# Merged SP transfers and a written SP order in an adaLN block with delta-rule attention and a mixture of experts

## The chip, the cores and the metric

The kernel runs on one core of a Trainium2 chip. The metric is the device time of one execution in microseconds. Lower is better.

The core has five engines that run at the same time, each with its own list of instructions, taken strictly in order: PE (matrix products; its weight loads are listed apart as PEld), DVE (vector work), ACT (activations), POOL (general elementwise work and indirect transfers) and SP, which here does nothing but begin transfers. A transfer is begun by an instruction on an engine's list, is carried out by 16 DMA engines that the whole core shares, and tells by a semaphore that it has landed. An instruction that waits for a semaphore holds up all that stands behind it on its engine.

## The reference

For x of 4 sequences of 1024 tokens with 256 features (all float32):

```python
mod = (_silu(L0_c) @ L0_wmod).reshape(B, 6, 1, -1)         # shifts, scales, gates sa ca ga sb cb gb
h = _layernorm(x) * (1 + ca) + sa
x = x + ga * attention(h)
h = _layernorm(x) * (1 + cb) + sb
x = x + gb * moe(h)

# attention: 16 heads of 64; q, k, v are projected, run through a causal convolution of 4 taps and silu
k = k / max(norm(k), 1e-12);  alpha = sigmoid(h Wa + ba);  beta = sigmoid(h Wb + bb)
def step(S, xs):                                           # a scan over the 1024 tokens
    v_old = S @ kt
    upd = vt - at * v_old
    S = clip(at * S + bt * outer(upd, kt), -5.0, 5.0)
    return S, S @ qt
y = y * silu(h Wg + bg);  out = y Wo

# moe: 8 experts of width 512, the two best of each token, softmax over the two, gelu
```

## The kernel before, in words

The scan is worked in chunks of 32 tokens of all four sequences (128 rows, `nch` = 32 chunks). Two chunks make a pair, and there are 16 pairs (`npair`). The function `chunks` runs over the pairs: while the two chunks of one pair pass through the recurrent state `S` (class `Chunk`), the next pair is prepared (class `Pair`). After the last pair, `blocks` runs the experts. Further functions (`rest`, `steps`, `experts`) stand behind conditions that are not met with these inputs.

The parts of a pair's work are Python generators, each with a letter: `k` keys and queries, `v` values and gates, `t` the triangular system, `s` the scaling of keys and queries (`scaled`), `c` the passes of the chunks with `outputs` and `finish`, `b` the bounds, `x` the loads of later rows of x, `z` the clearing of rows for the experts, and so on. The string `PLAN` gives the order in which they are advanced by one `yield` each, once a pair. That order is the written order. Line 379 sets `manual_schedule` for PE, DVE, ACT and POOL: their instructions stand in the program as written. SP is not in that set: there, a scheduler places the transfers by its own estimate of when each can begin.

All of the following transfers are begun on SP in the part that `chunks` builds, and their names are those in the profile:

- `w_kq`, `w_v`, `w_gt` (L428, L433, L436): the projections' weights, loaded anew in every pair from `in_w_qkv` and `in_w_g`, two head pairs ahead of their use. Each buffer is one of three (`w_kq`, `w_v`) or four (`w_gt`), so a load waits for the last product with the weights that lay there. `load_kq` makes two transfers, one for keys and one for queries, and `load_v` one for `w_v` and two for `w_gt`. `project` (L610) takes the weights, an activation (L619) begins the convolution, and three operations of DVE for each (L628) end it.
- `x` (L423): a chunk's rows of x. They are wanted in the order (sequence, half, token) and lie in HBM as (half, sequence, token), so `fill_x` makes eight transfers of 16 rows. Chunks 0 to 5 are loaded at the start, the others in `loads`, four chunks ahead of their pair's pass.
- `spread` to `g_scratch` (L900): the growth factors of a pair, which DVE makes in `triangle` (L894, L895), are written to HBM in four transfers, one for each sequence.
- `sc` from `g_scratch` (L994): in `scaled` they are read back, each row sent to 64 partitions. This happens four times a pair (queries and keys, even and odd chunk), with two transfers of 64 partitions each. POOL then multiplies (L1001), in two operations of 512 columns each, and copies `last` (L1004). `at_heads` gives the place in HBM.
- `x_scratch`, `out` (L1280, L1283): in `finish` a chunk's x after attention, which POOL has added (L1278), is stored, and then copied to `out` from HBM to HBM, its rows put in the other order.
- `u_scratch` (L1297) and `growth_scratch` (L735, L837): stores for the bounds.
- `rows_scratch` from `zero_row` (L1338): `clear` fills the experts' lists with blank rows, in 128-row parts, 18 parts a pair.

In the passes, POOL's `decayed` (L1231) makes `aS`, DVE adds the new part to it and gets `S` (L1196), and DVE's `yT` (L1252) takes the outputs out of PSUM.

The three buffers for PSUM results of most matmuls (`bank`) are taken in turn, so a product also waits until the one three before it has been read.

Of the kernel before, what the change touches and what calls it, by code (L numbers as in the profile page):

```python
# [32 lines left out]
F32 = mybir.dt.float32  # L33
# [3 lines left out]
ALU = mybir.AluOpType  # L37
# [3 lines left out]
B, D, C, NH, DH, KC = 4, 256, 1024, 16, 64, 4  # L41
HP = NH // 2
TC, TH, TE = 32, 16, 8
# [3 lines left out]
P = 128  # L47
RW = D + 8
# [313 lines left out]
def chunks(ctx, tc, a, nch, con, ones, modt, modc, x1_dram, rt, out):  # L362

    nc = tc.nc
    GA, SB, CB, GB = range(4)
    ident, iota8 = con["ident"], con["iota8"]
    npair = nch // 2
    wp = ctx.enter_context(tc.tile_pool(name="c_w", bufs=1))
    bp = ctx.enter_context(tc.tile_pool(name="c_buf", bufs=1))
    s1 = ctx.enter_context(tc.tile_pool(name="c_one", bufs=1))  # L370
    s2 = ctx.enter_context(tc.tile_pool(name="c_two", bufs=2))
    s3 = ctx.enter_context(tc.tile_pool(name="c_thr", bufs=3))
# [3 lines left out]


    E = mybir.EngineType
    ctx.enter_context(tc.manual_schedule(engines={E.PE, E.DVE, E.Activation, E.Pool}))

    is_open, done = {}, set()

    def take(pool, shape, name, tag=None, bufs=1, **more):
        tag = tag or name
        assert is_open.get(tag, 0) < bufs, tag
        is_open[tag] = is_open.get(tag, 0) + 1
        if bufs > 1:
            more["bufs"] = bufs
        return pool.tile(shape, F32, name=name, tag=tag, **more)

    def close(*tags):
        for tag in tags:
            is_open[tag] -= 1
            assert is_open[tag] >= 0, tag

    def need(*what):
        assert done.issuperset(what), what
# [3 lines left out]
    def bank(shape, name):  # L401
        banks[0] += 1
        return ps_g.tile(shape, F32, name=name, tag=f"g{banks[0] % 3}")

    half_p = lambda p: slice(p * 64, p * 64 + 64)
    quads = [slice(b * 32, b * 32 + 32) for b in range(B)]
# [6 lines left out]
    QC, KK, VC = 0, 1, 2  # L413

    x_of = {}

    def load_x(c, eng=nc.sync):
        x_of[c] = take(s3, [P, D], "x", bufs=9)
        fill_x(c, x_of[c], eng)

    def fill_x(c, x, eng):
        for there, here in by_batch(a["x"][c], x):
            eng.dma_start(here, there)  # L423

    def load_kq(hp):
        w = s3.tile([P, 2, 2, P], F32, name="w_kq")
        for x, i in ((KK, 0), (QC, 1)):
            nc.sync.dma_start(w[:, :, i], a["w_qkv"][:, :, x, hp])  # L428
        return w

    def load_v(hp):
        w = s3.tile([P, 2, P], F32, name="w_v", bufs=3)
        nc.sync.dma_start(w, a["w_qkv"][:, :, VC, hp])  # L433
        wg = s3.tile([P, 2, P], F32, name="w_gt", bufs=4)
        for p in range(2):
            nc.sync.dma_start(wg[:, :, half_p(p)], a["w_g"][:, :, p, hp * DH : (hp + 1) * DH])  # L436
        return w, wg

    w_next, v_next = [], []
# [166 lines left out]
    def project(w, h_t, x, hp, o):  # L606

        ps = bank([P, 2 * B, KC - 1 + TC], "ps_q")
        for dc in range(2):
            nc.tensor.matmul(  # L610
                ps.rearrange("p y t -> p (y t)"),
                lhsT=w[:, dc],
                rhs=h_t[:, dc].rearrange("p x b t -> p (x b t)"),
                start=(dc == 0),
                stop=(dc == 1),
            )
        taps = conv[:, x, hp]
        o = o.rearrange("p x b t -> p (x b) t")
        nc.scalar.activation(  # L619
            o, ps[:, :, 0:TC], AF.Identity, scale=taps[:, 0:1], bias=taps[:, KC : KC + 1]  # L620
        )
        return ps, taps, o

    def convolve(*projected):

        for j in range(1, KC):
            for ps, taps, o in projected:
                nc.vector.scalar_tensor_tensor(  # L628
                    o, ps[:, :, j : j + TC], taps[:, j : j + 1], o, op0=ALU.mult, op1=ALU.add
                )  # L630

    def silu(f):
        f = f.rearrange("p h x b t -> p (h x b t)")
        nc.scalar.activation(f, f, AF.Silu)

    def idle(n):
        for _ in range(n):
            yield

    class Pair:  # L640
# [100 lines left out]
        def keys_and_queries(self):  # L741
            need(("h", self.g), ("halo", self.g))
            kq = self.kq = take(s2, [P, 2, HP, 2, B, TC], "kq", bufs=2)
            for hp in range(HP):
                w = w_next.pop(0)
                w_next.append(load_kq((hp + 2) % HP))
                two = []
                for x, i in ((KK, 0), (QC, 1)):
                    two.append(project(w[:, :, i], self.h_t, x, hp, kq[:, i, hp]))
                    yield  # L750
                convolve(*two)
                yield
                if hp % 2:
                    for i in range(2):
                        silu(kq[:, i, hp - 1 : hp + 1])
                        if i and hp == HP - 1:
                            done.add(("kq", self.g))
                        yield
# [81 lines left out]
        def triangle(self):  # L840

            g, kq, dec, gam = self.g, self.kq, self.dec, self.gam
            need(("kq", g), ("dec", g))

            kk_r = self.kk_r = take(s1, [P, 32, TC], "kk_r")
            dq = self.dq = take(s2, [P, 32, TC], "dq", bufs=2)
            for par in range(2):
                two = [bank([P, HP, 2, TC], "ps_kk") for _ in range(2)]
                at = banks[0]
# [20 lines left out]
            kk = take(s1, [P, TC, TC], "kk")  # L870
# [22 lines left out]
            spread = s2.tile([P, 2, TC], F32, name="spread")  # L893
# [2 lines left out]
                spread[:, 0], spread[:, 1], -1.0, rk, op0=ALU.mult, op1=ALU.mult  # L896
            )

            for b, q in enumerate(quads):
                nc.sync.dma_start(g_dram[g][:, :, b].rearrange("w n t -> n w t"), spread[q])  # L900
            done.add(("spread", g))
            w_t = s1.tile([P, TC], F32, name="w_t")
            nc.vector.tensor_tensor(w_t, be, rk, ALU.mult)
# [27 lines left out]
            for x in range(2):  # L931
                at = [slice(x * TH + y * TE, x * TH + (y + 1) * TE) for y in range(2)]
# [45 lines left out]
        def scaled(self):  # L978


            g, kq = self.g, self.kq
            need(("M", g))
            kd = self.kd = take(s1, [P, 32, TC], "kd", tag="gam")
            nc.gpsimd.tensor_tensor(kd, self.dec, self.kk_r, ALU.mult)
            close("kk_r")
            yield
            need(("kt", g), ("spread", g))
            close("arep")
            self.last = []
            for w in (1, 0):  # L990
                for par in range(2):
                    sc = take(s1, [P, HP, B, TC], "sc", tag=("kk", "kk_r")[par])
                    for p in range(2):
                        nc.sync.dma_start(  # L994
                            sc[half_p(p)].rearrange("q h b t -> q (h b t)"),
                            at_heads(g, w, p, par).partition_broadcast(DH),
                        )
                    yield
                    for h4 in range(0, HP, 4):
                        o = kq[:, w, h4 : h4 + 4, par]  # L1000
                        nc.gpsimd.tensor_tensor(o, o, sc[:, h4 : h4 + 4], ALU.mult)  # L1001
                    if w == 1:
                        last = take(s3, [P, B, HP], "last", bufs=3)
                        nc.gpsimd.tensor_copy(last.rearrange("q b h -> q h b"), sc[:, :, :, TC - 1])  # L1004
                        self.last.append(last)
                    close(("kk", "kk_r")[par])
                    if (w, par) == (0, 1):
                        done.add(("scaled", g))
                    yield
# [38 lines left out]
    def at_heads(g, w, p, par):  # L1048

        n = p * 16 + par * 8  # L1050
        return g_dram[g][w, n : n + 8].rearrange("n b t -> (n b t)")

    def of_pair(w, g):

# [271 lines left out]
            yield  # L1326


    g_dram = nc.dram_tensor("g_scratch", [npair, 2, 32, B, TC], F32, kind="Internal").ap()

    rows = rt.rows[: NE * rt.room].rearrange("(e n p) d -> n p e d", e=NE, p=P)
    blank = iter([(n, e) for n in range(nch + BL // P) for e in range(NE)])
    blanks = []

    def clear(count):

        for _, (n, e) in zip(range(count), blank):
            one = nc.sync.dma_start(rows[n][:, e], rt.zero)  # L1338
            for other in rt.sent:
                apart(tc, one, other)  # L1340
            blanks.append((n, one))

    def clears():
        for _ in range(6):
# [45 lines left out]

    def loads(first):
        for c in range(first, min(first + 2, nch)):
            load_x(c)
            yield

    def both_of(pair, prev):
# [75 lines left out]
    def later_loads():  # L1472

        yield from idle(1)
        for c, x in unread:
            fill_x(c, x, nc.sync)
            yield
            if c > 2:
                yield
        nc.sync.dma_start(rw, a["router"])  # L1480
        for p in range(2):
            for x in range(2):
                nc.sync.dma_start(
                    w_o[half_p(p)].rearrange("q (h x) d -> q x h d", x=2)[:, x],
                    a["w_o"][half_p(x), :, p],
                )
        yield
# [17 lines left out]
    for g in range(npair):  # L1505
# [4 lines left out]
        if g + 1 < npair:  # L1510
            x = newer
# [895 lines left out]
```

## Time and profile before

| | |
|---|---|
| time, median of 3 executions | 1919.11 us (1913.41 to 1926.53) |
| the profiled execution: time, span | 1922.9 us, 1921.1 us |
| mean granted clock of TensorE | 0.919 |
| busy: PE, PEld, DVE, ACT, POOL | 1632.0, 1297.1, 1482.3, 826.7, 716.4 us |
| transfers begun on SP, largest groups | rows_scratch 272, w_kq 260, w_gt 260, x 248, w_v 130, sc 128, u_scratch 128 |
| moved by the DMA engines | 249.52 MB, mean 130 GB/s |

The profile is of one execution. The span goes from the first instruction to the last, and the time of an execution is a little more. A line of the timeline or of a group names the source line, the engine, the operation and its tiles (out<-in); a line of SP (SPq) is an instruction that begins a transfer, and its length is the time it holds the queue, not the time until the data have landed. In brackets stands how long the engine was idle before and what, as far as the semaphores tell, ended that. A line of waits says who waited for whom: microseconds in total, how often, and the longest.

### The profile page before, as it was taken

To read this page: it belongs to the slowest core of one execution; us is meant where nothing else is said; L and a number is where in the kernel's file an instruction comes from. 1 tells how busy PE (TensorE), PEld (TensorE's weight loads), DVE (VectorE), ACT (ScalarE), POOL (GpSimd) and SP (SyncE) were. 2 spreads that over 40 slices of the span, in tenths; PEclk is the share of its full clock that TensorE was granted. 3 is DMA by queue.
4 is the path that set the end of the run, shared out by engine and by line. 5 is a ranking of instruction groups with operands and counts; after the bars stand their busy time and mean duration, and the time that the engine had idled before them with its cause. 6 is when DMAs were issued, how large, how long until landed. Compare 5 with 4: busy or idle time off the path is not lost.

```text
span 1921.1 us, 88201 instructions
## 1 busy us (share of the span) xinstructions
PE 1632.0 (85%) x38610; PEld 1297.1 (68%) x38610; DVE 1482.3 (77%) x3622; ACT 826.7 (43%) x1652; POOL 716.4 (37%) x913
## 2 busy tenths in 40 slices
PE   5578999889989898989898989898888675989994
PEld 3456676667676766767676767676667564878883
DVE  4678797968788888878787978797968335789973
ACT  3344545444545544545445444554443112334331
POOL 1032343424342525252534343433424432454343
PEclk9889998989999998989899989998989677999997
DMA  4455444443545445354535453636343216788882
GB/s 117 127 161 129 105 108 94 107 109 95 148 115 141 123 120 137 107 134 111 146 103 150 106 153 97 161 94 153 110 112 112 56 36 207 187 208 219 231 231 35
DMA packets 431490, 249.52 MB, mean 130 GB/s; under 512 B 242996, under 2 KB 410808, under 8 KB 430840
## 3 DMA queue, kind: packets, MB, share of 16 engines
q1 hardware_dynamic: 416488, 223.65, 43.6%
q0 software_dynamic: 13664, 18.38, 5.2%
q8 instruction: 306, 5.01, 1.1%
q10 hardware_dynamic: 944, 1.77, 0.3%
q14 instruction: 88, 0.72, 0.1%
HBM read 165.99 MB, written 81.87 MB: 129 GB/s over the span
## 4 chain that ended last, share of the span: by engine, by line
PE 66%; DVE 11%; issue 7%; POOL 5%; SPq 5%; DMA 4%; ACT 3%; POOLq 0%; DVEq 0%; ACTq 0%
PE ps_q L610 22%; PE ps_hm L2116 6%; PE ps_yb L2129 6%; PE ps_w L1265 5%; PE ps_gt L780 4%; PE ps_u L1149 3%; PE ps_kk L853 3%; PE ps_o L1208 2%; PE ps_z L1127 2%; SPq L423 2%; PE ps_t L1031 2%; PE ps_s L1187 2%; DMA sc<-g_scratch 2%; PE ps_t L1019 2%; DVE kq L628 2%
## 5 line engine op out<-in xcount | busy, mean ns | idle before, releaser
L628 DVE SCALAR_TENSOR_TENSOR kq<-ps_q,w_conv,kq 128x256 f32<-128x256 f32 x768 | 319.7, 476 | 150.2 <-ACT kq L619 149.6
L610 PE MATMUL ps_q<-hT,w_kq 128*128 128x280 f32 x1024 | 323.2, 460 | 58.9 <-issue 20.6
L610 PEld LDWEIGHTS ps_q<-hT,w_kq 128*128 128x128 f32 x1024 | 203.5, 213 | 125.9 <-issue 58.2
L619 ACT ACTIVATE kq<-ps_q,w_conv 128x256 f32<-128x256 f32 x256 | 142.4, 563 | 234.8 <-PE ps_q L610 233.1
L1001 POOL TENSOR_TENSOR kq<-kq,sc 128x512 f32<-128x512 f32 x128 | 163.5, 1299 | 143.6 <-DMA sc<-g_scratch 116.5
L2136 POOL DMA_INDIRECT out<-yb,at_b x72 | 120.4, 1672 | 190.2 <-DVE gate L2106 48.7
L628 DVE SCALAR_TENSOR_TENSOR v<-ps_q,w_conv,v 128x256 f32<-128x256 f32 x384 | 158.9, 476 | 41.9 <-ACT v L619 41.7
L1231 POOL TENSOR_TENSOR aS<-S,last 128x1024 f32<-128x1024 f32 x64 | 122.5, 1914 | 135.9 <-DVE S L1196 133.4
L780 PE MATMUL ps_gt<-hT,w_gt 128*128 128x256 f32 x512 | 144.3, 410 | 29.6 <-issue 20.5
L787 ACT ACTIVATE gate<-ps_gt,b_gt 128x256 f32<-128x256 f32 x128 | 60.5, 473 | 239.3 <-PE ps_gt L780 239.1
L610 PE MATMUL ps_q<-hT,w_v 128*128 128x280 f32 x512 | 153.5, 441 | 11.6 <-issue 4.7
L2116 PE MATMUL ps_hm<-hT,w 128*128 128x256 f32 x576 | 136.4, 392 | 7.6 <-issue 5.9
L2123 ACT ACTIVATE hm<-ps_hm,b 128x256 f32<-128x256 f32 x144 | 68.2, 474 | 167.5 <-issue 120.4
L2129 PE MATMUL ps_yb<-w,hm 128*128 128x256 f32 x576 | 130.3, 379 | 0.0
L2116 PEld LDWEIGHTS ps_hm<-hT,w 128*128 128x128 f32 x576 | 112.7, 197 | 25.9 <-issue 8.9
L610 PEld LDWEIGHTS ps_q<-hT,w_v 128*128 128x128 f32 x512 | 97.7, 204 | 47.3 <-issue 13.1
L780 PEld LDWEIGHTS ps_gt<-hT,w_gt 128*128 128x128 f32 x512 | 92.0, 194 | 53.1 <-issue 28.5
L1265 PE MATMUL ps_w<-w_o,yT 128*128 128x256 f32 x512 | 121.0, 391 | 4.3 <-DVE yT L1252 2.8
L1278 POOL TENSOR_TENSOR x<-x,add 128x256 f32<-128x256 f32 x32 | 29.0, 905 | 236.4 <-DVE add L1276 232.3
L2129 PEld LDWEIGHTS ps_yb<-w,hm 128*128 128x128 f32 x576 | 106.7, 190 | 13.4 <-DVE yb L2134 0.3
L1265 PEld LDWEIGHTS ps_w<-w_o,yT 128*128 128x128 f32 x512 | 98.2, 195 | 20.1 <-DVE yT L1252 3.0
L619 ACT ACTIVATE v<-ps_q,w_conv 128x256 f32<-128x256 f32 x128 | 71.3, 573 | 93.7 <-PE ps_q L610 93.7
(265 smaller groups left out, 3230.5 us busy)
## 6 DMA issues: line engine op xcount, KB each, us to landing
w<-in_w SPq DMA_DIRECT2D x72, 512.0 KB
rows_scratch<-zero_row SPq DMA_DIRECT2D x272, 132.0 KB
w_kq<-in_w_qkv SPq DMA_DIRECT2D x260, 128.0 KB
sc<-g_scratch SPq DMA_DIRECT2D x128, 256.0 KB
w_v<-in_w_qkv SPq DMA_DIRECT2D x130, 128.0 KB
w_gt<-in_w_g SPq DMA_DIRECT2D x260, 64.0 KB
u_scratch<-u SPq DMA_DIRECT2D x128, 128.0 KB
hb<-rows_scratch SPq DMA_DIRECT2D x36, 264.0 KB
```

Source lines behind the costliest of these rows:

```text
L610: nc.tensor.matmul(ps.rearrange("p y t -> p (y t)"), lhsT=w[:, dc], rhs=h_t[:, dc].rearrange("p x b t -> p (x b t)"), start=(dc == 0), sto ...
L619: nc.scalar.activation(o, ps[:, :, 0:TC], AF.Identity, scale=taps[:, 0:1], bias=taps[:, KC : KC + 1])
L628: nc.vector.scalar_tensor_tensor(o, ps[:, :, j : j + TC], taps[:, j : j + 1], o, op0=ALU.mult, op1=ALU.add)
L780: nc.tensor.matmul(ps, lhsT=wg[:, dc], rhs=self.h_t[:, dc, :, :, KC - 1 :].rearrange("p x b t -> p (x b) t"), start=(dc == 0), stop=(dc == 1),
L787: nc.scalar.activation(gate[:, hp].rearrange("p x b t -> p (x b t)"), ps.rearrange("p y t -> p (y t)"), AF.Silu, bias=b_gt[:, hp : hp + 1],)
L1001: nc.gpsimd.tensor_tensor(o, o, sc[:, h4 : h4 + 4], ALU.mult)
L1231: nc.gpsimd.tensor_tensor(aS.rearrange("q b h i -> q (b h) i"), S[:, bs].rearrange("q b h i -> q (b h) i"), self.pair.last[self.par][:, bs ...
L1265: nc.tensor.matmul(ps_w, lhsT=self.yT[:, hp].rearrange("q b t -> q (b t)"), rhs=w_o[:, hp], start=(hp == 0), stop=(hp == HP - 1),)
L2116: nc.tensor.matmul(ps, lhsT=self.w1[:, dc, fc * P : (fc + 1) * P], rhs=self.hT[:, dc], start=(dc == 0), stop=(dc == 1),)
L2123: nc.scalar.activation(self.hm[:, fc], ps, AF.Gelu, bias=self.b1[:, fc : fc + 1])
L2129: nc.tensor.matmul(ps, lhsT=self.hm[:, fc, s * P : (s + 1) * P], rhs=self.w2[:, fc], start=(fc == 0), stop=(fc == 3),)
L2136: return nc.gpsimd.indirect_dma_start(out=places, out_offset=bass.IndirectOffsetOnAxis(ap=self.at[:, s : s + 1], axis=0), in_=y, in_offset ...
```

## The change

SP joins the engines whose instructions stand in written order. Transfers are merged: one for `w_kq`, one for `w_gt`, one for `spread`, one for each run of blank rows that lie in the same 128-row part. From chunk 6 on, x is first copied from HBM to HBM in the wanted order (`reorder_x`, two chunks ahead of the load), and then loaded by one transfer. `g_scratch` now has the sequence ahead of the head, so that `spread` can go in one transfer; `sc` therefore lies as (sequence, head, token) in its 64 partitions and is filled in pieces of 1 KB, and POOL reads it with the two outer indices exchanged.

```diff
-    ctx.enter_context(tc.manual_schedule(engines={E.PE, E.DVE, E.Activation, E.Pool}))
+    ctx.enter_context(tc.manual_schedule(engines={E.PE, E.DVE, E.Activation, E.Pool, E.SP}))
...
+    x_rows = nc.dram_tensor("x_rows", [nch, P, D], F32, kind="Internal").ap()
+
+    def reorder_x(c):
+
+        if 6 <= c < nch:
+            nc.sync.dma_start(
+                x_rows[c].rearrange("(b h t) d -> b h (t d)", b=B, h=2),
+                a["x"][c].rearrange("(h b t) d -> b h (t d)", b=B, h=2),
+            )
+
     def load_kq(hp):
         w = s3.tile([P, 2, 2, P], F32, name="w_kq")
-        for x, i in ((KK, 0), (QC, 1)):
-            nc.sync.dma_start(w[:, :, i], a["w_qkv"][:, :, x, hp])
+        nc.sync.dma_start(w, a["w_qkv"][:, :, : KK + 1, hp])
         return w
...
-        for p in range(2):
-            nc.sync.dma_start(wg[:, :, half_p(p)], a["w_g"][:, :, p, hp * DH : (hp + 1) * DH])
+        nc.sync.dma_start(
+            wg.rearrange("x c (p i) -> x c p i", p=2), a["w_g"][:, :, :, hp * DH : (hp + 1) * DH]
+        )
...
-                    two.append(project(w[:, :, i], self.h_t, x, hp, kq[:, i, hp]))
+                    two.append(project(w[:, :, x], self.h_t, x, hp, kq[:, i, hp]))
...
-            for b, q in enumerate(quads):
-                nc.sync.dma_start(g_dram[g][:, :, b].rearrange("w n t -> n w t"), spread[q])
+            nc.sync.dma_start(g_dram[g].rearrange("w b n t -> (b n) w t"), spread)
...
-                    sc = take(s1, [P, HP, B, TC], "sc", tag=("kk", "kk_r")[par])
+                    sc = take(s1, [P, B, HP, TC], "sc", tag=("kk", "kk_r")[par])
                     for p in range(2):
                         nc.sync.dma_start(
-                            sc[half_p(p)].rearrange("q h b t -> q (h b t)"),
+                            sc[half_p(p)].rearrange("q b h t -> q b (h t)"),
                             at_heads(g, w, p, par).partition_broadcast(DH),
                         )
                     yield
                     for h4 in range(0, HP, 4):
                         o = kq[:, w, h4 : h4 + 4, par]
-                        nc.gpsimd.tensor_tensor(o, o, sc[:, h4 : h4 + 4], ALU.mult)
+                        nc.gpsimd.tensor_tensor(
+                            o, o, sc[:, :, h4 : h4 + 4].rearrange("q b h t -> q h b t"), ALU.mult
+                        )
...
-                        nc.gpsimd.tensor_copy(last.rearrange("q b h -> q h b"), sc[:, :, :, TC - 1])
+                        nc.gpsimd.tensor_copy(last, sc[:, :, :, TC - 1])
...
-        return g_dram[g][w, n : n + 8].rearrange("n b t -> (n b t)")
+        return g_dram[g][w, :, n : n + 8].rearrange("b n t -> b (n t)")
...
-    g_dram = nc.dram_tensor("g_scratch", [npair, 2, 32, B, TC], F32, kind="Internal").ap()
+    g_dram = nc.dram_tensor("g_scratch", [npair, 2, B, 32, TC], F32, kind="Internal").ap()
...
-        for _, (n, e) in zip(range(count), blank):
-            one = nc.sync.dma_start(rows[n][:, e], rt.zero)
+        some = [at for _, at in zip(range(count), blank)]
+        for n in sorted({n for n, _ in some}):
+            es = [e for m, e in some if m == n]
+            k = len(es)
+            one = nc.sync.dma_start(
+                rows[n][:, es[0] : es[0] + k], rt.zero.unsqueeze(1).to_broadcast([P, k, RW])
+            )
             for other in rt.sent:
                 apart(tc, one, other)
-            blanks.append((n, one))
+            blanks.extend([(n, one)] * k)
...
     def loads(first):
         for c in range(first, min(first + 2, nch)):
-            load_x(c)
+            reorder_x(c + 2)
+            x_of[c] = take(s3, [P, D], "x", bufs=9)
+            nc.sync.dma_start(x_of[c], x_rows[c])
             yield
...
         nc.sync.dma_start(rw, a["router"])
+        for c in (6, 7):
+            reorder_x(c)
         for p in range(2):
```

## The prediction

> **What bounds the kernel now.** I read the page first, for the engines' shares and the chain; then the waits, for who stops whom; then one pair of chunks instruction by instruction, on SP, POOL, DVE and PE; then the table by stage.
>
> ```profile
> span 1921.1 us, 88201 instructions
> ...
> PE 1632.0 (85%) x38610; PEld 1297.1 (68%) x38610; DVE 1482.3 (77%) x3622; ACT 826.7 (43%) x1652; POOL 716.4 (37%) x913
> ...
> PE 66%; DVE 11%; issue 7%; POOL 5%; SPq 5%; DMA 4%; ACT 3%; POOLq 0%; DVEq 0%; ACTq 0%
> ```
>
> PE carries two thirds of the chain, the SP queue and DMA 9% together (some 170 us). Chain shares are no savings: behind a removed link stands whatever was nearly as late. Hence the stage. Fifteen stretches of about 91 us (130 to 1495 us) each handle one pair; this is pair 7, for which the columns are the length and then the busy times of PE, PEld, DVE, ACT and POOL:
>
> ```profile
> 672.00:764.00 92.00, 83.30 (x2298) 64.62 (x2298) 74.92 (x182) 44.25 (x87) 36.27 (x50) 0.93 0.49 128
> ```
>
> PE idles 8.7 us of 92: no shortening of transfers can give more there. What SP does in that pair, in order of time (start, length):
>
> ```profile
> 723.88 1.75 SPq L900 DMA_DIRECT2D g_scratch<-spread  x4
> 725.73 0.55 SPq L433 DMA_DIRECT2D w_v<-in_w_qkv  x1
> 726.37 2.12 SPq L436 DMA_DIRECT2D w_gt<-in_w_g  x2
> 728.59 0.56 SPq L433 DMA_DIRECT2D w_v<-in_w_qkv  x1
> 729.20 1.26 SPq L436 DMA_DIRECT2D w_gt<-in_w_g  x2
> 730.50 5.49 SPq L423 DMA_DIRECT2D x<-in_x  x8
> 736.03 1.13 SPq L994 DMA_DIRECT2D sc<-g_scratch  x2
> ```
>
> The first `sc` needs only `spread`, yet ten microseconds of issuing (weights, eight pieces of x) stand between. What that costs, on POOL, DVE and PE:
>
> ```profile
> 740.71 2.71 POOL L1001 TENSOR_TENSOR kq<-kq,sc 128x512 f32<-128x512 f32 x2 [6.36 <-PE ps_q L610]
> ...
> 746.15 1.92 POOL L1231 TENSOR_TENSOR aS<-S,last 128x1024 f32<-128x1024 f32 x1
> ```
>
> ```profile
> 748.10 1.22 DVE L1196 TENSOR_TENSOR S<-ps_s,aS 128x1024 f32<-128x1024 f32 x1 [0.93 <-POOL aS L1231]
> ```
>
> ```profile
> 750.07 4.07 PE L610 MATMUL ps_q<-hT,w_kq 128*128 128x280 f32 x8 [1.17 <-DVE yT L1252]
> ```
>
> POOL idles 6.36 us before the first product with `sc` (the named releaser is wrong: the second half of `sc` lands at 740.55). POOL works in order, so aS is late, DVE waits 0.93 us for it, PE 1.17 us for DVE. Six microseconds shrink to one because DVE is full until 747.17. Over the run:
>
> ```profile
> POOL kq L1001 <- DMA sc<-g_scratch: 116.5, 32, 12.0
> ...
> DVE S L1196 <- POOL aS L1231: 15.4, 10, 2.9
> ...
> PE ps_q L610 <- DVE yT L1252: 14.5, 9, 2.8
> ```
>
> The first row is the idle time of an engine that is 37% busy, the last is what reaches PE: nine waits of 0.57 to 2.79 us, all in pairs 5 to 13. In pairs 1 to 3, 14 and 15 SP had begun sc early and DVE never waits for aS.
>
> **The change, part by part.** *Issues.* By the trace an SP issue takes 0.42 (x) to 0.61 us (w_kq, w_gt; medians), with 0.05 between. Per pair there were 100: 16 w_kq, 8 w_v, 16 w_gt, 16 x, 18 zero rows, 8 sc, 8 u, 4 spread, 6 others. After: 8, 8, 8, 4 (two reorders, two x), about 7.5, 8, 8, 1 and 6, so 58. At 0.6 that is 60 us of SP down to 35. That is SP's own time, not the end's.
>
> *The path of sc.* In written order: spread at 723.88, one issue (0.43); the zero rows, which the old schedule had put ahead of spread (0.5); w_v, w_gt, w_v, w_gt (0.56+0.61 twice); reorder (0.69, as out<-x_scratch of L1283, the same pattern); x (0.42). With seven gaps that ends at 728.6: sc's halves begin at 728.6 and 729.2 instead of 736.0 and 736.6. Landing took 4.3 us (median of 128), so 733.5 for 740.6. POOL is free at 734.36 (end of x at L1278) and begins its product there, 6.35 us earlier. Product 2.7, last 0.4; the scatter in between needs DVE's `at` (737.3) and ends at 739.9; aS ends at 741.8, not 748.07. DVE comes to L1196 at 747.17: the wait is gone, 5.4 us to spare. What is late next: DVE itself, then PE's preceding ps_t, which ends at 748.90. So of PE's 1.17 us 0.93 are won. The lesser of both gaps, pair by pair (1.57, 0.92, 0.93, 2.05, 0.89, 2.79, 1.77, 0.57, 2.44), sums to 13.9; pair 4 has 0.9 on DVE that hardly shows on PE. I take 14.
>
> *Unknown prices.* The merged issues (more dimensions) lie between 0.36 (x1 store) and 1.04 us (w_ab); I take 0.65, nearest in shape; at 1.04 sc comes 0.8 us later, inside the 5.4. The new sc moves the same 256 KB in pieces of 1 KB, not 4 KB: hb (264 KB in 1056 B pieces) lands in 3.5 us, the slowest old sc in 5.8; I take 4.3, and 5.8 is inside too. POOL now reads sc in runs of 32: Tr at L972 reads runs of 16 and takes 1.07 us for the same 512 elements, the strided copy at L1004 0.24 us for 32 single elements; the product stays between 1.07 and some 1.4 us, taken 1.27. It would touch the path above 3.4 us. Fewer weight transfers: laid pair after pair in written order on the old times, each load but one (see the start) lands 4 us or more ahead of its matmul, so they gain and lose nothing. Without that lead a late load costs PE its lateness.
>
> *The reorder transfers.* [...] The row: out<-x_scratch has the same outermost dimension of 4, posts its landing from 4 DMA engines and lands in 4.0 us, against 2.7 for the store of the same 128 KB by rows. [...] By the trace a reorder has a whole pair (90 us) before x is read, and x is read 25 us or more after it lands, so the cover is wide and I charge nothing.
>
> *Written order.* Which SP transfers move? In pairs 4 to 13 nearly none: zero rows stood 4 places early, x1's store 4 late. Now SP stands at the x1 store until POOL's x, then 2.7 us for its landing before out; sc's second pair waits behind both and lands at 742.0 instead of 742.9; POOL wants it at 742.3. In the loop's other half the next w_kq goes from 780.9 to 785.6, lands at 789.4, PE wants it at 796.5. In pairs 1 to 3, 14 and 15 the second sc comes 3 to 7 us later, just as POOL comes to it. Price: 0.
>
> *The start.* At 46.25 w_kq is begun behind the four w_o, and PE waits 7.05 us for it. The merges save four issues that count, but SP now stands at an earlier w_kq until 27.1 while five x pieces used to go first, and two reorders come before w_o. So w_kq begins 0.7 us later and has 256 KB more ahead of it (w_o's 1 MB took 9.7 us, so 2.4 at most): 0.7 below, 3 above, taken 1.5. At 118 us a w_kq that had been begun at 73.8 stands behind toks, gates and sc and lands at 122.1 for 120.4: 0 to 1.7, taken 0.8.
>
> **Sum.** 1922.9 (the profiled execution; span 1921.1) − 14 + 1.5 + 0.8 = 1911.2, or −11.7 us. That execution lies 3.8 above the median of 1919.1, so 1907.4.
>
> **Rivals.** *More comes back.* PE also has stalls that nothing visible ends ("issue"), between 60 and 1500 us: 22.5 us at ps_q, 20.5 at ps_gt, 17.0 at ps_z, 12.1 at ps_t, 10.4 at ps_kk, 82 in all. If they come from crowded DMA rings and 42% fewer requests free a third, 27 us more: 1907.4 − 27 = 1880. For: the chain's 9%. Against: the bytes stay the same and the queue's share of the DMA engines (43.6%) with them. *Nothing comes back.* The queue was all but in written order already, and PE's wait for yT may give way to its wait for ab_r just before (12.0 us, 11 times, 1.1 each): 1919 to 1922. Against: that wait ends at 747.65, before the one removed. *Slower.* SP stands at the x1 store in the loop's second half, the w_kq behind it is late. It decides from a lag of 7.1 us beyond what I worked out; beyond it each microsecond costs 14 us, once a pair. At 2.4 over: 1907 + 34 = 1941. For: x1 landings reach 5.3 us, and stores, u and a_t stand there in a row. Against: even that leaves 4 us.
>
> **How the numbers follow.** Forecast 0.60 (own range 1897 to 1916), more 0.18, nothing 0.10, slower 0.12. This kernel's runs spread over 0.7%, so about 1% can be told from no change: under 1900 or over 1938. Faster by that: most of "more" and a tenth of the forecast, 0.25; slower 0.12; the same 0.63. The range from 1882 to 1930 holds the forecast's own with the unknown prices, the case of nothing, and some two thirds of "more"; it leaves out the rest of that (0.06) and the slower case (0.12).
>
> **What would show it.** Right: POOL's wait for sc (116.5 us) falls below 50; DVE's for aS (15.4) and PE's for yT (14.5) below 4 each; L1001 stays near 1.27 us; SP shows one L900 and two L423 per chunk; the first sc comes within 6 us of spread. Wrong: new waits of PE for w_kq, L1001 above 2 us, or a first sc that still comes ten microseconds after spread.

## The result and the profile after

The changed kernel takes 1974.34 us (median of 4 runs, 1972.2 to 1980.91) where the kernel before took 1916.26 us beside it: a ratio of 1.031, 95% interval 1.025 to 1.036. It is slower by 3%. The forecast was 1907.4 us with a range from 1882 to 1930. Medians here and below are of all executions, while the ratios leave out those that fell into a slower state, so a ratio is not the quotient of the medians beside it.

The page of the changed kernel, the lines shown of the kernel before:

```profile
span 1970.0 us, 87417 instructions
...
PE 1659.4 (84%) x38610; PEld 1318.7 (67%) x38610; DVE 1498.6 (76%) x3622; ACT 826.3 (42%) x1652; POOL 722.2 (37%) x913
...
PE 71%; DVE 10%; issue 8%; ACT 4%; DMA 4%; POOL 2%; SPq 2%; POOLq 0%; DVEq 0%; ACTq 0%
```

SP and POOL have all but left the chain (2% each, 5% before), as intended. But PE, which runs the same 38,610 matmuls, is busy for 27.4 us more, and the span grew by 48.9: the other 21.5 us are idle time of PE. So two things have to be found, longer idle time and slower matmuls.

The waits over the run name the first (line L1030 is L1019 of before, the product of Tn and kd into ps_t; L790 is L780; L1010 is L1001):

```profile
POOL kq L1010 <- DMA sc<-g_scratch: 129.3, 42, 10.7
...
PE ps_t L1030 <- issue: 42.1, 17, 4.8
...
PE ps_gt L790 <- issue: 29.7, 12, 6.8
```

PE's nine waits for yT (14.5 us) and DVE's ten for aS (15.4) are gone from the list altogether. In their place PE stands at L1030 for 42.1 us and at L790 for 29.7 us that nothing visible ends. The kernel before had

```profile
PE ps_gt L780 <- issue: 20.5, 9, 5.2
...
PE ps_t L1019 <- issue: 12.1, 9, 3.5
```

One such stall, on PE in the pair after the one that the prediction walked through:

```profile
774.89 1.39 PE L1030 MATMUL ps_t<-Tn,kd 32*32 32x16 f32 x128 [1.07 <-ACT ab_r L715]
776.20 2.15 PE L620 MATMUL ps_q<-hT,w_kq 128*128 128x280 f32 x8
778.29 0.71 PE L1030 MATMUL ps_t<-Tn,kd 32*32 32x16 f32 x62
781.87 1.09 PE L1030 MATMUL ps_t<-Tn,kd 32*32 32x16 f32 x66 [2.87 <-issue]
```

The stall falls between the 62nd and the 63rd of a run of equal matmuls, whose two operands are whole tiles and had been there for the 62. So a wait for data does not fit that place. Counted from each pair's first w_kq matmul the place moves: matmul 70 in this pair, then 24, 106, 60, 14, 96 and 50 in the next six, that is 46 earlier each time, in steps round 128. 128 matmuls with their loads are 256 instructions, and the page's instruction queue moved 306 packets of 16 KB for some 78,000 instructions of PE, one packet for about 255. PE stands at packet boundaries: it waits for its own instructions. The trace has the packet too: one of 16 KB on that queue runs from 779.13 to 780.53, begun 0.13 us after PE had stopped, and PE goes on 1.34 us behind its end. In all 15 such stalls of over 0.9 us at these products PE goes on 1.2 to 1.6 us behind the end of a packet of that queue. Why the packets come late is argued from what follows; no run takes the fetches away.

Why there? What SP does at the same moment:

```profile
771.49 0.33 SPq L847 DMA_DIRECT2D growth_scratch<-k_t  x1
771.92 2.70 SPq L1003 DMA_DIRECT2D sc<-g_scratch  x4
774.66 0.62 SPq L437 DMA_DIRECT2D w_kq<-in_w_qkv  x1
775.39 1.64 SPq L1352 DMA_DIRECT2D rows_scratch<-zero_row  x3
777.12 8.46 SPq L1308 DMA_DIRECT2D u_scratch<-u  x4
```

and what the kernel before did at the same work:

```profile
747.57 0.55 SPq L837 DMA_DIRECT2D growth_scratch<-k_t  x1
748.21 3.86 SPq L994 DMA_DIRECT2D sc<-g_scratch  x4
752.13 1.24 SPq L428 DMA_DIRECT2D w_kq<-in_w_qkv  x2
753.48 3.05 SPq L1338 DMA_DIRECT2D rows_scratch<-zero_row  x6
756.63 3.83 SPq L1297 DMA_DIRECT2D u_scratch<-u  x4
```

The order is the same. But sc's second half, w_kq and 792 KB of zero rows were begun within 5.1 us instead of 8.3. The windows of the 8 us from the first of these products, before and after (the last three columns are the granted clock, the busy share of the DMA engines and GB/s):

```profile
747.60:755.60 8.00, 6.78 (x251) 5.24 (x255) 4.98 (x9) 1.13 (x2) 5.69 (x8) 0.61 0.76 190
```

```profile
774.90:782.90 8.00, 5.13 (x264) 4.28 (x264) 5.47 (x11) 1.13 (x2) 4.64 (x4) 0.87 1.08 246
780.80:787.60 6.80, 5.05 (x74) 3.51 (x73) 0.73 (x2) 1.16 (x2) 4.21 (x7) 0.50 0.86 172
```

The DMA engines go from three quarters busy to full (at 1.08 some of the packets overlap). In eight of the nine pairs 4 to 12 all of sc's second half is begun before the products start, as here; in the kernel before, in none. The second line of the last fence is the second cost: from within the stall on, PE's clock is 0.50 for 6.8 us. The clock records (88 before, 100 after) hold only 1.0 and 0.5, and those at 0.5 add up to 314 us before and 376 after (mean clock 0.919 and 0.905). In the changed kernel a w_kq matmul takes 0.40 us at 1.0 and 0.67 at 0.5 (medians of 848 and 151). By these two an estimate of the loss in the extra 62 us is 41%, 25 us, which is about PE's extra busy time of 27.

By stages (starts of PE's w_kq groups in both traces): pair 1 starts 6.4 us later, the 14 pairs from there to pair 15 lose 27.1, the end of the chunks 11.7, the experts 3.

### The profile page after: what moved, and what is told of

Same layout as the page of the kernel before. It is cut to its first block, busy times and chain, and to the rows that moved or that the text cites. A ratio compares the mean times of both kernels' runs of the same rounds, so it can differ in the third digit from the quotient of the medians.

```text
span 1970.0 us, 87417 instructions
## 1 busy us (share of the span) xinstructions
PE 1659.4 (84%) x38610; PEld 1318.7 (67%) x38610; DVE 1498.6 (76%) x3622; ACT 826.3 (42%) x1652; POOL 722.2 (37%) x913
## 4 chain that ended last, share of the span: by engine, by line
PE 71%; DVE 10%; issue 8%; ACT 4%; DMA 4%; POOL 2%; SPq 2%; POOLq 0%; DVEq 0%; ACTq 0%
PE ps_q L620 21%; PE ps_gt L790 6%; PE ps_hm L2136 6%; PE ps_w L1276 6%; PE ps_yb L2149 5%; PE ps_o L1219 3%; PE ps_s L1198 3%; PE ps_u L1160 3%; PE ps_kk L863 3%; PE ps_t L1030 3%; PE ps_t L1042 2%; PE ps_o L1178 2%; PE ps_z L1138 2%; DVE v L638 2%; DMA out<-yb,at_b 2%
## 5 line engine op out<-in xcount | busy, mean ns | idle before, releaser
L638 DVE SCALAR_TENSOR_TENSOR kq<-ps_q,w_conv,kq 128x256 f32<-128x256 f32 x768 | 319.5, 476 | 190.8 <-ACT kq L629 189.6
L620 PEld LDWEIGHTS ps_q<-hT,w_kq 128*128 128x128 f32 x1024 | 205.5, 215 | 117.9 <-issue 48.9
L1010 POOL TENSOR_TENSOR kq<-kq,sc 128x512 f32<-128x512 f32 x128 | 164.1, 1302 | 138.5 <-DMA sc<-g_scratch 129.3
L638 DVE SCALAR_TENSOR_TENSOR v<-ps_q,w_conv,v 128x256 f32<-128x256 f32 x384 | 159.1, 476 | 30.8 <-ACT v L629 30.7
L790 PE MATMUL ps_gt<-hT,w_gt 128*128 128x256 f32 x512 | 149.8, 424 | 33.8 <-issue 29.7
L620 PE MATMUL ps_q<-hT,w_v 128*128 128x280 f32 x512 | 148.8, 430 | 11.6 <-ACT Tt L1055 3.3
L790 PEld LDWEIGHTS ps_gt<-hT,w_gt 128*128 128x128 f32 x512 | 96.0, 202 | 57.3 <-issue 34.1
L2126 DVE SCALAR_TENSOR_TENSOR gate<-gates,share,gate 128x256 f32<-128x256 f32 x216 | 104.4, 483 | 6.2 <-ACT gate L2122 1.2
```

The source lines that it names most:

```text
L620: nc.tensor.matmul(ps.rearrange("p y t -> p (y t)"), lhsT=w[:, dc], rhs=h_t[:, dc].rearrange("p x b t -> p (x b t)"), start=(dc == 0), sto ...
L638: nc.vector.scalar_tensor_tensor(o, ps[:, :, j : j + TC], taps[:, j : j + 1], o, op0=ALU.mult, op1=ALU.add)
L790: nc.tensor.matmul(ps, lhsT=wg[:, dc], rhs=self.h_t[:, dc, :, :, KC - 1 :].rearrange("p x b t -> p (x b) t"), start=(dc == 0), stop=(dc == 1),
L1010: nc.gpsimd.tensor_tensor(o, o, sc[:, :, h4 : h4 + 4].rearrange("q b h t -> q h b t"), ALU.mult)
L2126: nc.vector.scalar_tensor_tensor(self.gate[:, s], gates[:, b], self.share[:, s, b : b + 1], self.gate[:, s], op0=ALU.mult, op1=ALU.add,)
```

## The experiments

Two theories stood at the outset. A, crowding: the merged transfers are begun in half the time, fill the DMA engines beside the small products, and PE's instructions come late. B, standing in order: SP stands at the spread and x1 stores and what is behind comes late. C and D came up with the first results: C, that sc's new pieces cost by themselves; D, that an early sc makes POOL run without a break and block DVE. E, in the third and fourth group, joins A and D: the harm comes from sc being early. All ratios are to the kernel before on the same chip, with 95% intervals.

**Taking the change apart.** First the order alone, on the kernel before:

```
-manual_schedule(engines={E.PE, E.DVE, E.Activation, E.Pool})
+manual_schedule(engines={E.PE, E.DVE, E.Activation, E.Pool, E.SP})
```

> The kernel before with one change: SP's instructions keep the written order too. Theory A (crowding): the loss of the change (about 55 us) comes from the merged transfers, which are issued in half the time and so fill the DMA engines just when PE runs the small products into ps_t (kd by Tn), where it uses up instructions fastest; its 16 KB instruction fetches come late there (idle put down to issue at that line 42 us after, 12 before). With single transfers the issues stay spread, so A expects 1912 to 1938 us, issue at that line below 22 us, and PE at half clock for less than 335 us (314 before, 376 after). Theory B (standing in order): SP stands at the spread store and at the x1 store and everything behind comes late; it expects most of the loss here, 1945 to 1985 us, since a hundred issues in strict order stand worse than 58.

Measured (e1): 1941.39 us, ratio 1.010 (1.007 to 1.013). Issue idle at the products was 15.8 us, as A said, but half-clock time was not low (362.6 us) and the time a little above A's 1938 and below B's 1945. What the trace shows is the opposite of the change: with a hundred issues in strict order the first sc begins 14 us behind spread instead of 11.6, and PE's waits for yT double, 13.7 us more where the loss is 19:

```profile
PE ps_q L610 <- DVE yT L1252: 28.2, 10, 3.8
```

Then the merges alone, the same line undone in the changed kernel.

> The changed kernel with SP's order given back to the scheduler: merged transfers alone. Theory A (crowding): the zero rows, w_kq and u still follow sc's second pair closely, so most of the loss stays: 1945 to 1975 us, issue at the kd by Tn line above 28 us. Theory B (standing in order): the loss is gone and the gain that was predicted shows: 1895 to 1920 us, issue there near 12 us.

Measured (e2): 1998.58 us, ratio 1.040 (1.037 to 1.043), worse than the whole change and above A's 1975 (issue idle at the products 33.9 us, above 28 as A said). B is dead: the written order is not what makes it slow, in the company of the merges it even helps by 1%. It also showed the loss in its crudest form. sc now begins 3.5 us behind spread, and on DVE and POOL one reads, for one pair:

```profile
1065.68 4.92 DVE L952 TENSOR_TENSOR X<-X,rk 128x64 f32<-128x64 f32 x1
```

```profile
1065.87 1.92 POOL L1242 TENSOR_TENSOR aS<-S,last 128x1024 f32<-128x1024 f32 x1
1067.71 0.22 POOL L1081 COPY hT<-hT 128x24 f32<-128x24 f32 x1
1067.87 0.21 POOL L1102 COPY hT<-hT 128x24 f32<-128x24 f32 x1
1068.03 2.48 POOL L1010 TENSOR_TENSOR kq<-kq,sc 128x512 f32<-128x512 f32 x2
1070.46 0.22 POOL L1015 COPY last<-sc 128x32 f32<-128x32 f32 x1
```

```profile
1074.42 1.19 PE L790 MATMUL ps_gt<-hT,w_gt 128*128 128x256 f32 x2 [5.26 <-issue]
```

A DVE multiplication of 64 elements a partition takes 4.92 us instead of 0.22 and ends with POOL's run, 0.1 us before its last copy does. DVE is then late for its six operations that read ps_q and free a PSUM bank (L638, from 1072.28 on), and PE, which stood for 5.26 us, goes on with ps_gt at 1074.42. That DVE ended this wait is argued from the order. "Issue" hides that too: 63.6 us at this group over the run, and most of its long stalls do not lie at the packet boundaries. The minimum, median and longest of that DVE line, of the merges alone and of the changed kernel:

```profile
L952 DVE TENSOR_TENSOR X<-X,rk x32: 224/1148/4967, 97.7 to 1562.5; 128x64 f32<-128x64 f32 x32
```

```profile
L952 DVE TENSOR_TENSOR X<-X,rk x32: 224/225/2236, 100.9 to 1521.7; 128x64 f32<-128x64 f32 x32
```

In the changed kernel eight of the 32 take over 1.5 us, and POOL is busy for 96% or more of each of the eight. In the rows above DVE's operation (4.92 us) lasts as long as six POOL instructions in a row, so here it did not get in between them. Why DVE stands while POOL runs is not shown; that POOL holds it up is argued from these times.

Single zero rows in the changed kernel (the old `clear`):

> The changed kernel with one transfer per zero row and expert again (18 of 132 KB a pair instead of about 7.5 larger). Theory A (crowding): the largest lump in the kd by Tn stretch is thinned, six rows take 3 us to issue instead of 1.6 and w_kq and u move behind them: a third to a half of the loss comes back, 1940 to 1960 us, issue at that line 20 to 32 us. Theory B (standing in order): ten more issues a pair in the same order give nothing back: 1965 to 1990 us.

Measured (e3): 1953.09 us, ratio 1.015 (1.011 to 1.019): half of the loss comes back, as A said. But issue idle at the products was 39.5 us in its profile (its longest execution, 1969.26 us), where A wanted 20 to 32.

The old sc (layout of the scratch, four spread stores, 4 KB pieces, POOL in order):

> The changed kernel with spread, sc and the scratch between them as before: four spread stores instead of one, sc read in pieces of 4 KB instead of 1 KB, POOL reading sc in its own order. Theory A (crowding) says the bytes are the same and sc is not the lump: 1960 to 1980 us, within 1% of the change. Theory C (small pieces): four times as many packets of sc hold up instruction fetches, above all in the kd by Tn stretch, which sc's second two transfers precede by 1 to 3 us: 1935 to 1955 us, issue at that line below 28 us. Theory B: 1.5 us more of SP a pair, 1970 to 1985.

Measured (e4): 1934.42 us, ratio 1.006 (1.002 to 1.010). The time is that of C, to a microsecond, and a miss for A; but issue idle at the products, 32.9 us, did not fall below C's 28.

**Does each part cost by itself?** The parts put alone into the kernel before, or taken alone from the change:

```
e5: kernel before + new spread, g_scratch and sc      e6: kernel before + merged clear()
e7: changed kernel, loads() with load_x(c) again      e8: changed kernel, old sc and old clear()
```

> The kernel before with the new sc alone: one spread store, the scratch turned, sc read in 1 KB pieces, POOL reading it in runs of 32; SP's order left to the scheduler. The old layout took 2.4% off the changed kernel. Theory C (the pieces or POOL's way of reading cost by themselves): the same 2% here, 1950 to 1970 us. Theory D (sc does no harm alone; coming early, it lets POOL run aS and the products without a break and DVE's X times rk, which has two inputs in SBUF, stands until POOL pauses, 4.7 us for 0.2): as much as the scheduler brings sc forward, 1915 to 1945 us, excess of X times rk above 20 us if slow and below 15 if not. Theory A (crowding by lumps alone): no change, 1910 to 1928 us.

> The kernel before with merged zero rows alone (7.5 instead of 18 a pair). Theory A (crowding): the lump is there without the rest, 1930 to 1950 us, issue idle at the kd by Tn line 20 to 32 us (12 before). Theory D: no effect on POOL or DVE, 1912 to 1928 us.

> The changed kernel with x loaded in eight pieces a chunk again, without the reorder through DRAM (16 x issues a pair instead of 4, 3.4 MB less moved). Theory A: the reorder runs on four engines in packets of 16 KB away from the kd by Tn stretch, so little comes back: 1955 to 1975 us. If its packets hold up instruction fetches: 1935 to 1955 us. SP has 5 us more to issue ahead of the first sc; theory D expects that this alone breaks POOL's run and gives 10 to 20 us back.

> The changed kernel with old sc and single zero rows: written order, merged w_kq and w_gt, reorder. If the two prices add (46 us for sc, 28 for the rows), it comes to 1895 to 1910 us and beats the kernel before. If they are two names for one crowding and the second gives little once the first is gone: 1920 to 1940 us, near the order alone (1941).

Measured, in that order (e5 to e8): 1937.06 us, 1.007 (1.004 to 1.010); 1928.75 us, 1.002 (1.000 to 1.005); 1945.22 us, 1.012 (1.008 to 1.016); 1917.00 us, 0.997 (0.994 to 0.999). So C fell as an account of the loss: the new sc, whose removal gave back 2.4% of the changed kernel, costs 0.7% alone, the rows cost 0.2% instead of 1.6%, and even x in eight pieces, which gives SP more to do, gave back 1.8%. A missed e5 and e7. e6 falls between D (to 1928) and A (from 1930), with issue idle at the products at 23.0 us, as A said. D, with its collisions, allowed for e5, but for at most 20 of the 29 us of e7. e7 lies where its expectation blamed the reorder's packets, a rival that is weighed below; e8 lies between its two cases. Whatever part is taken out, much of the loss goes. What the parts share is that each part of the change brings the first sc forward. Its median lag behind spread (pairs 1 to 14) is 11.6 us before, 5.5 in the change, 9.4 with x in eight pieces, 7.3 with the old sc, 8.7 in the fourth run, which is the one that beats the kernel before.

That fourth run is where the predicted gain went. Between pair 1 and pair 15 it takes 1277.6 us for 1291.1 of the kernel before, 13.5 less where 14 were forecast, and its waits for yT are gone too. That figure is a net one: over the run half-clock time is 19 us shorter than before, PE's idle time at packet boundaries 12 us longer. So how near it comes to 14 is in part chance. Its sc, w_kq and rows:

```profile
752.19 4.90 SPq L1004 DMA_DIRECT2D sc<-g_scratch  x4
757.13 0.65 SPq L437 DMA_DIRECT2D w_kq<-in_w_qkv  x1
757.89 3.85 SPq L1348 DMA_DIRECT2D rows_scratch<-zero_row  x6
```

9.5 us again for what the change begins in 5.1. The reason is in `scaled`: the four sc share two buffers. When POOL is late with the first two, SP must stand at the fourth until POOL frees its buffer, and that paces everything behind it. When sc comes early POOL has freed both, and SP runs through. SP's waits for POOL at sc, of the kernel before, the change and e8 (`last` is the copy behind POOL's products with an sc):

```profile
SPq L994 <- POOL last L1004: 34.9, 15, 3.5
```

```profile
SPq L1003 <- POOL last L1015: 4.8, 7, 1.2
```

```profile
SPq L1004 <- POOL last L1014: 26.5, 13, 2.6
```

**Where lumps stand, and what sc's pieces do.**

```
e9:  changed kernel; a pair's first two clear(3) moved to just ahead of nc.sync.dma_start(x1_dram[c], x1)
e10: e8 + two stores of 396 KB of zeros to a scratch, a pair, beside the products
e11: e8 + the same two stores ahead of the x1 store
e12: changed kernel, old sc, but spread stored by two transfers instead of four
```

> The changed kernel with the first two of a pair's six clears (two or three of its 7.5 zero-row transfers, 792 KB) begun just ahead of the first x1 store instead, some 28 us after the kd by Tn products begin, where PE uses 0.2 to 0.6 instruction lines in 4 us instead of 1.2. Nothing else moves. Theory A (lumps beside the products make the instruction fetches late, and each long stall is followed by half clock): idle put down to issue at the kd by Tn line falls from 42 to under 25 us and the time to 1935 to 1958 us. Theory B (standing in order): the x1 store and what stands behind it come later, nothing comes back: 1970 to 1990 us.

> The kernel with old sc, single zero rows and the rest of the change (1917 us) with two further stores of 396 KB of zeros to a scratch of their own in each of 15 pairs, begun where the kd by Tn products run. Theory A: issue idle at that line from its 20 or so to above 35 us, the time up by 20 to 45 us, 1937 to 1962 us. Rival (extra bytes are hidden wherever they stand): 1912 to 1925 us.

> The same two further stores of 396 KB a pair, begun ahead of the first x1 store, some 28 us later, where PE uses few instructions. Theory A: at most a third of what they cost beside the products, 1915 to 1930 us. Rival (the bytes cost wherever they stand, by the load on the memory): the same as beside the products, within 6 us.

> The changed kernel with the old scratch layout, so that sc is read in 4 KB pieces and POOL reads it in order, but spread stored by two transfers instead of the four that the old layout had. Theory C (1 KB pieces and POOL's order are what costs): as with the old layout and four stores, 1928 to 1945 us. Theory E (it was the two or three issues that four stores put ahead of sc, that is, its lateness by 1.5 us): halfway, 1945 to 1965 us.

Measured: e9 1959.13 us, 1.019 (1.014 to 1.025), 1.1% back. The time is at the edge of what A said, but issue idle at the products stayed at 35.5 us where A wanted under 25: moving the rows helps without emptying that place. e10 1934.30 us, 1.003 (0.999 to 1.008), and e11 1922.70 us, 1.000 (0.997 to 1.004): 0.7% and 0.4% above the kernel without them. The order is A's, but the intervals overlap, so that a lump costs more beside the products than elsewhere is not shown by this pair. A's 20 to 45 us beside the products are refuted, and so is its sign, issue idle above 35 us (20.5): in the kernel where SP waits for POOL at sc, 792 KB more cost little. e12 1962.04 us, 1.019 (1.013 to 1.025), against 1.006 with four stores: the same layout and the same pieces, two issues fewer ahead of sc, and 1.3% slower, inside what E said and outside C. Its first sc comes 6.2 us behind spread (7.3 with four stores), SP waits 2.9 us for POOL at sc (12.1), and sc's second half is begun before the products in eight of nine pairs (six).

**Is it sc's being early?** Eight stores of 256 bytes a pair are added to the changed kernel, once ahead of the first sc, once (the control) at the x1 store, where SP stands idle; then two combined repairs.

```
+for i in range(8):
+    nc.sync.dma_start(tiny[i : i + 1], rt.zero[:1, :64])
e13: ahead of the first sc     e14: ahead of the x1 store
e15: e8 with its first six zero rows at the x1 store     e16: e13 and e9 together
```

> The changed kernel with eight further stores of 256 bytes a pair, begun ahead of the first sc: nothing is taken away, SP has 3 to 4 us more to do and sc comes that much later (lag behind spread 5.5 to about 9 us, where the fast version without the new sc and rows has 8.7). Theory E (early sc lets POOL free both buffers at once, so that SP begins sc's second half, w_kq, zero rows and u in one run beside the kd by Tn products, and POOL's unbroken run holds up DVE's X times rk): pairs of the early kind fall from 8 of 9 to 3 or fewer, X times rk's excess from 20 to under 10 us, and the time to 1935 to 1955 us, faster for more work. Theory A alone (lumps, whatever sc's time): no change, 1965 to 1985. Theory B (SP's standing): slower, 1980 to 2000.

> Control: the same eight tiny stores a pair, begun ahead of the first x1 store, where SP stands idle. sc is not delayed. Theory E: as the changed kernel, within 0.5% (1965 to 1985 us). If the tiny stores themselves did something, this would move as the run with them ahead of sc does.

> The version with old sc and single zero rows (0.997 of the kernel before), with the first six zero rows of a pair begun ahead of the first x1 store instead of beside the products. Theory A (lumps beside the products): another 5 to 15 us, 1900 to 1912 us, ratio 0.988 to 0.994. If sc's pacing alone decides: no change, 1912 to 1920.

> The changed kernel with all its merged transfers and both repairs: eight tiny stores that delay sc, and the first two clears of a pair at the x1 store. If the two halves of the account are separate, their gains add (20 us each): 1920 to 1940 us. If the lump matters only while sc is early, the delay gives nearly all and the moved rows little: 1935 to 1950 us.

Measured: e13 1961.01 us, 1.016 (1.012 to 1.020); e14 1978.40 us, 1.027 (1.023 to 1.032). The intervals are apart: more work for SP makes the kernel faster by about 1% if, and only if, it delays sc (lag 9.1 us; 5.4 in the control). SP's wait for POOL at sc is back with the delay, and not in the control:

```profile
SPq L1012 <- POOL last L1024: 30.6, 15, 2.8
```

```profile
SPq L1010 <- POOL last L1022: 0.9, 2, 0.6
```

The time is 6 us above E's range, the control inside it. DVE's line shows the collision gone, at most 1.26 us (the line is L959 there):

```profile
L959 DVE TENSOR_TENSOR X<-X,rk x32: 224/226/1256, 101.2 to 1512.7; 128x64 f32<-128x64 f32 x32
```

and three of nine pairs have all of sc's second half begun before the products, for eight in the changed kernel. But issue idle at the products, 28.5 us, fell only by a third, and 21.8 us appeared at the next group (6.6 in the change), so this run does not say that fewer late instructions made the gain. What fell is the time by which X times rk exceeds its usual 0.225 us: 5 us over the run, for 21 in the change and 22 in the control.

e15 1926.07 us, 1.000 (0.997 to 1.003): no gain over the 0.997 without it, above both its cases and a miss for A. e16 1948.52 us, 1.008 (1.004 to 1.011): of the change's 3.1% the delay gives back 1.4, the moved rows 1.1, both 2.3. The two halves very nearly add, as the first case of its expectation said, though its median came out 9 us above that case and inside the second.

## Why the prediction was wrong

*Right.* The path of the first sc. Forecast: 4.7 us behind spread (728.6 less 723.88); measured 5.1 in that pair (spread at 744.81, sc at 749.90). Issues 58 a pair: 58.4. The merged issues at 0.65: 0.37 (spread) to 0.67 (reorder). POOL's product 1.27: 1.30. The waits for aS and yT, 15.4 and 14.5: both gone. sc's landing was too low at 4.3 us (median of 128 now 5.1, longest 7.6), though the median stays inside the 5.8 allowed for. The reorder's landing 4.0: 4.2 us, and little is left as its price: taking it away gave back 1.8%, delaying sc without taking it away 1.4%, and the two intervals overlap. And the 14 us, for which the fourth run of the second group shows 13.5, net of other changes.

*The step that failed* is "what is late next". The prediction followed POOL's gained 6.35 us to aS, DVE and PE, and stopped there: DVE had 5.4 us to spare, so all was well. It did not follow the same gain back to SP, to whom an earlier POOL hands both sc buffers, nor to DVE, whose X times rk stands while POOL runs without a break. The prediction put these at nothing. The price of an early sc was missing from the sum: 1.1% (e14 less e13), 1.3% (e12 less e4) or 1.4% (the change less e13) of the time, 21 to 27 us. The profile of before had shown it twice, in pairs 3 and 14, which the prediction names among those where SP begins sc early and DVE does not wait for aS. In pair 3, on DVE and then on PE:

```profile
368.17 4.91 DVE L943 TENSOR_TENSOR X<-X,rk 128x64 f32<-128x64 f32 x1
```

```profile
376.91 2.04 PE L780 MATMUL ps_gt<-hT,w_gt 128*128 128x256 f32 x4 [5.15 <-issue]
```

It counted the wait that those pairs lack and not the one that they have.

*"At 0.6 that is 60 us of SP down to 35. That is SP's own time, not the end's."* SP's own time fell as forecast in kind (61 to 44 us a pair, mean of pairs 1 to 14, with the waits inside its issues). That it is not the end's was wrong: the same bytes begun in two thirds of the time filled the DMA engines while they lasted (1.08 for 0.76 in the windows above). The zero rows at that place were worth another 1.1% (e9). The remaining 0.8% of e16 is about what the new sc costs alone (0.7%); that these are the same is only argued.

*"Written order. Price: 0."* Alone it costs 1.0%, by a late sc; in company it gains 1%. The two were priced apart, and neither number holds for the other.

*POOL's wait for sc below 50 us:* 129.3. It did not go, it moved. In the pair shown it is 1.53 us at the first product (6.36 before) and 7.25 us at the third, whose sc stands behind k_t. POOL's idle time cost nothing in either place; it was a poor sign to name.

*The start:* forecast +1.5, measured 6.4. The wait for w_kq was sized right (8.2 for 7.1 us); beside the rest stands a lower clock, 38 us at half instead of 22 up to pair 1; that it makes up the rest is argued.

*The rivals.* "More comes back" had the wrong sign: with fewer requests, issue idle of PE rose from 117 to 150 us over the run (sum of PE's rows). Sorted by place in PE's instruction stream (a boundary at every 256th), 62 us before and 91 after lie at the packet boundaries, so nearly all of the rise is there. "Slower" had the wrong place: the profile lists a wait of PE for w_kq only at the start. The mechanism found here stood in no rival.

*What stays open.* How the loss splits between late instructions, DVE held up by POOL and the clock. The delay of sc (e13) took away DVE's stands, 5 us for 21, and left PE's idle time at packet boundaries, 98 us for 91; the moved rows (e9) left both, 22 and 87 us. The clock follows the time: over all executions its mean is 0.905 in the change and about the same in e14, 0.912 in e13, 0.908 in e9, 0.925 in e8. Each trace is of one execution, and the control's is its fastest, 1961.41 us, as long as that of e13, so the traces of these two do not show where the gain of 1.1% arose. A kernel with X times rk out of POOL's way was not tried, and the 11.7 us at the end of the chunks were not taken apart.

## What to carry to other kernels

When a transfer comes earlier, follow the buffers that its reader frees back to the queue: a wait for a buffer may be what spaces the transfers behind it (here SP's 34.9 us at sc, 4.8 in the change). Fewer and larger transfers were not lighter ones here; ask what else runs in the microseconds in which they now meet (here the DMA engines went from 0.76 to 1.08 in 8 us). A gain of one wait removed and a loss of another made can both be real, so test the parts alone and together; here the version without the new sc and the merged rows keeps the gain, 0.3% under the kernel before.

## What the runs showed of the hardware

In the changed kernel stalls of PE and half clock stand together. The 2.87 us stall began at 779.0, and the clock was halved from 780.8 to 787.6; between 130 and 1495 us 32 of 35 halved stretches follow 1.0 to 3.3 us of idle time of PE within the 3.41 us before them (0.7 to 0.8 in the others), and all last a multiple of 3.41 us. The idle time does not settle it alone: 1.0 to 1.7 us stand before 13 of the 35, and before no halving in 12 other windows of 3.41 us. That a stall brings the half clock, and so costs more than itself, is argued from this order; no run shows it apart.

The instruction packets, 306 of 16 KB in either kernel, were not hidden behind PE's work. PE stood for up to 4.8 us at the places where one ends, 62 us in the kernel before and 91 in the changed one, and 42 us at the products alone, where in the pair shown it used 264 matmuls in 8 us with the share of the DMA engines at 1.08.
